# Between attention and the experts: the last tile's jobs first, blank rows on three queues, later biases, more idle transposes

## The chip, the cores and the metric

One core of one Trainium2 chip runs the whole kernel. The metric is the time of one execution on the device in microseconds (us); a profiled execution also has a span, from its first to its last instruction. The engines are PE (TensorE), DVE (VectorE), ACT (ScalarE), POOL (GpSimd) and SP (SyncE); SP, ACT and POOL issue DMAs.

## What is computed

A layer of graph attention and a layer of experts, for N = 4096 nodes of width D = 512, all in float32:

```python
def layer(x, adj, Wks, Wqs, Wvs, Wo, Wg, bg, W1, b1, W2, b2):
    n = layernorm(x)
    q, k, v = (einsum('nd,hdk->hnk', n, W) for W in (Wqs, Wks, Wvs))   # 8 heads of 64
    s = einsum('hqk,hmk->hqm', q, k) * 64 ** -0.5
    s = s + 0.01 * eye - 1e16 * (1 - maximum(adj, eye))                # mask
    x = x + einsum('hqm,hmk,hko->qo', softmax(s), v, Wo)
    f = layernorm(x)
    logits = f @ Wg + bg                                               # 8 experts
    top, idx = top_k(logits, 2)
    w = softmax(top)
    y_e = gelu(f @ W1[e] + b1[e]) @ W2[e] + b2[e]                      # for each expert e
    return x + sum over the two chosen experts of w * y_e
```

## The kernel before

`_fast` works in stages, with P = 128 rows to a tile and 32 tiles (i = 0 to 31). Its order of instructions on every engine is that in which the program writes them.

**Projections and lists.** Keys and values of all nodes go to the table `kv_d` in DRAM, queries to `q_d`, and for every tile of queries a list is made of the nodes that it attends to.

**Attention** runs over pairs of steps, `duos`, S of them. For a tile, each step gathers rows of `kv_d` into a ring (POOL), transposes the keys, and computes scores, exponentials and values. After a tile's last pair, `end_of(i, n)` registers what is left to do for it under later step numbers, with `at(n, job)`; the loop over n takes all jobs registered for n after the pair's own work. When the pairs are used up (n >= S), the loop goes on with n until no jobs are left, so from there on only the jobs remain.

For one tile the jobs are: `scale` (division by the softmax sums), `flip_o` (PE transposes to `po`, ACT copy to `oT`), `project` (PE, L823) and `residual` (DVE adds x, L832, the sum is stored to `out`, L834, and its statistics are taken). Routing follows, by groups of tiles: tiles 0 to 27 go four at a time, then group 7 is tiles 28 and 29, group 8 is tile 30 and group 9 is tile 31. `route(g, n)` registers `root` (one over the standard deviation, DVE), `norm` (ACT, scales x in place, L885), `flip` (PE, ACT), `gate` (PE L905, DVE adds the bias, L909), `rank` and `place` (DVE), `number_places` (PE), `keep_places` (DVE, L949), `pick` twice and `weigh` (DVE, one exponential on ACT, L994), `finish` (DVE) and `scatter`: an indirect DMA on POOL (L1012) that writes each row to the place of its expert in the table `xs_d`, twice per tile. A 1x1 memset `tick` stands ahead of each such DMA.

The steps of the last tiles overlap. From S on they hold, in the order of registration:

| step | jobs |
|---|---|
| S | `rank`, `place` of group 7; `norm` of 8; `flip_o` of tile 31 |
| S+1 | `number_places`, `keep_places` of 7; `flip` of 8; `project`, `residual` of 31 |
| S+2 | `pick`, `weigh` of 7; `gate` of 8; `root` of 9 |
| S+3 | `finish` of 7; `rank`, `place` of 8; `norm` of 9 |
| S+4 | `scatter` of tile 28; `number_places`, `keep_places` of 8; `flip` of 9 |
| S+5 | `scatter` of 29; `pick`, `weigh` of 8; `gate` of 9 |
| S+6 | `finish` of 8; `rank`, `place` of 9 |
| S+7 | `scatter` of 30; `number_places`, `keep_places`, `totals` of 9 |
| S+8, S+9, S+10 | `pick`, `weigh`; `finish`; `scatter` of 31 |

**Totals and blank rows.** `xs_d` gives each of E = 8 experts a region of R = 4224 rows. `totals` counts the rows of each expert, computes `ends` (the first free row of each region, one copy per partition with the partition's number added, L958), and writes 128 blank rows behind each region's last row: eight indirect DMAs on POOL (L964), so that the last tile of every expert has defined rows.

**Tables.** After the jobs, DVE and PE work out from the counts, for each of up to 71 row tiles, its expert and its first row, and put them in `table` (L1125 to L1163). A check of the softmax sums follows, which ends in `flag` (L1179).

**Experts.** `fetch(b)` loads the first row's number from `table` into a register of SP and reads 128 rows of `xs_d` (L1204), so it has to wait for all scatters and blank rows. `bb`, the second biases of all experts copied to all partitions (2 MB), is loaded on ACT's queue ahead of them (L1192); it lies where tiles of the stage before lay. `warm` is 36 transposes of the identity, whose result nobody reads (L1210). `turn(b)` transposes the rows (L1215), `hidden(b)` is the first product (L1227), `turn_hidden` transposes it and applies GELU, `second` is the second product (L1251), adds `bb` (L1263), scales and adds the result to `out` with an accumulating indirect DMA on POOL (L1265). 69 row tiles are always run. The experts' weights, W1 and W2, are loaded on SP's queue into the ring as attention leaves it, and the last of them (L1086, `w`) at step S.

Of the kernel before, what the change touches and what calls it, by code (L numbers as in the profile page):

```python
# [20 lines left out]
P = 128  # L21
# [54 lines left out]
def _fast(ctx, tc, dram, flag, x, adj, Wks, Wqs, Wvs, Wo, Wg, bg, W1, b1, W2, b2, out):  # L76
    nc = tc.nc
# [242 lines left out]
    with ExitStack() as s1:  # L320
# [52 lines left out]
        def norm(i):  # L373
            mv, rstd = mvs.pop(i)
            nc.vector.reciprocal(rstd, rstd)
            xns[i] = work.tile([P, D], F32, tag="xn", name=f"xn_{i}")
            nc.vector.tensor_scalar(
                xns[i], xts.pop(i), mv[:, 0:1], rstd, op0=ALU.subtract, op1=ALU.mult
            )
# [249 lines left out]
    with ExitStack() as s2:  # L629
# [45 lines left out]
        rows_ = 0  # L675
        later = {}

        def at(n, job):
            later.setdefault(n, []).append(job)

        def gather(s, x):
            st = steps[s]
# [115 lines left out]
        def end_of(i, n):  # L798

            hold = {}  # L800

            def scale():
                o = os_[i][:, :, : NP * VW].rearrange("p b (h v) -> p b h v", v=VW)
                r = inverses[:, i].rearrange("p (b h) -> p b h", b=2)
                nc.vector.reciprocal(r, o[:, :, :, KD])
                on = mid.tile([P, 2, NP, KD], F32, tag="on", name=f"on_{i}")
                nc.vector.tensor_mul(
                    on, o[:, :, :, :KD], r.unsqueeze(3).to_broadcast([P, 2, NP, KD])
                )
                hold["on"] = on.rearrange("p b h v -> p (b h v)")  # L810

            def flip_o():
                pt = bank(f"po_{i}", [NP, P])
                for c in range(NP):
                    nc.tensor.transpose(pt[:, c, :], hold["on"][:, ts(c, P)], ident)
                oT = mid.tile([P, NP, P], F32, tag="oT", name=f"oT_{i}")
                nc.scalar.copy(oT, pt)
                hold["oT"] = oT

            def project():  # L820
                hold["py"] = bank(f"py_{i}", [D])
                for c in range(NP):
                    nc.tensor.matmul(  # L823
                        hold["py"], hold["oT"][:, c, :], wo[:, c, :],
                        start=(c == 0), stop=(c == NP - 1),
                    )

            def residual():
                g = group_of[i]
                m = groups[g]  # L830
                xi = xs_[i][:, :D]
                nc.vector.tensor_add(xi, xi, hold["py"])  # L832
                queue = nc.sync if i < NT - 3 else nc.scalar
                queue.dma_start(out=out[ts(i, P), :], in_=xi)  # L834
                if g not in gst:
                    gst[g] = small.tile([P, 2, 4], F32, tag="mvg", name=f"mvg_{g}")
                k = m.index(i)
                stats = small.tile([P, nc.vector.BN_STATS_DIM], F32, tag="stats", name=f"sb_{i}")
                nc.vector.bn_stats(stats, xi)
                nc.vector.bn_aggr(gst[g][:, :, k], stats)  # L840

            scale()
            at(n + 1, flip_o)
            at(n + 2, project)
            at(n + 2, residual)
            g = group_of[i]
            if i == groups[g][-1]:
                route(g, n + 3)

        def route(g, n):  # L850
# [32 lines left out]
            def norm(k):  # L883
                xi = xs_[m[k]]
                nc.scalar.activation(  # L885
                    xi[:, :D], xi[:, :D], AF.Identity, bias=hold["shift"][:, k : k + 1],
                    scale=hold["y"][:, k : k + 1],
                )
                nc.gpsimd.iota(xi[:, D : D + 1].bitcast(I32), pattern=[[0, 1]],
                               base=m[k] * P, channel_multiplier=1)  # L890

            def flip(k):
                i = m[k]
                pt = bank(f"px_{i}", [DC, P])
                for c in range(DC):
                    nc.tensor.transpose(pt[:, c, :], xs_[i][:, ts(c, P)], ident)
                xT = mid.tile([P, DC, P], F32, tag="x2T", bufs=2, name=f"x2T_{i}")
                nc.scalar.copy(xT, pt)
                hold["xT", k] = xT

            def gate(k):
                i = m[k]
                pl = bank(f"pl_{i}", [E])
                for c in range(DC):
                    nc.tensor.matmul(  # L905
                        pl, hold["xT", k][:, c, :], wg[:, c, :],
                        start=(c == 0), stop=(c == DC - 1),
                    )
                nc.vector.tensor_add(hold["l"][:, k, :], pl, bg_sb)  # L909
# [44 lines left out]
            def totals():  # L954
                pn = bank("pn", [E])
                nc.tensor.matmul(pn, ones, count, start=True, stop=True)
                ends = tail.tile([P, E], I32, name="ends")
                nc.vector.tensor_add(ends, pn, pad_e)  # L958
                number = tail.tile([P, E], I32, name="number")
                nc.vector.tensor_scalar_add(number, pn, float(P - 1))  # L960
                closing["number"] = number
                for e in range(E):
                    nc.gpsimd.memset(tick, 0.0)
                    s = nc.gpsimd.indirect_dma_start(  # L964
                        out=xs_d,
                        out_offset=bass.IndirectOffsetOnAxis(ap=ends[:, e : e + 1], axis=0),
                        in_=blank, in_offset=None,
                    )
                    for t in scatters:
                        tc.declare_no_dep(s.ins, t.ins, reason="other rows")  # L970
                    scatters.append(s)
# [48 lines left out]
                    tc.declare_no_dep(s.ins, t.ins, reason="other rows")  # L1020
                scatters.append(s)

            at(n, root)
            n += 1
            for k in range(G):
                at(n + k // 2, lambda k=k: norm(k))
                at(n + k // 2 + 1, lambda k=k: flip(k))
                at(n + k // 2 + 2, lambda k=k: gate(k))
            n += (G - 1) // 2 + 3
            at(n, rank)  # L1030
            at(n, place)
            at(n + 1, number_places)
            at(n + 1, keep_places)
            if g == len(groups) - 1:
                at(n + 1, totals)
            at(n + 2, lambda: pick(0))
            at(n + 2, lambda: pick(1))
            at(n + 2, weigh)
            at(n + 3, finish)
            n += 4  # L1040
            for k in range(G):
                for j in range(2):
                    at(n + k, lambda k=k, j=j: scatter(k, j))

        AHEAD = 5
        tick = small.tile([1, 1], F32, bufs=1, name="tick")
# [53 lines left out]
        while n < S or any(k >= n for k in later):  # L1100
            duo(scores, n + 1)
            duo(values, n)
            if n < S:
                end = steps[duos[n][-1]]
                if end["last"]:
                    end_of(end["i"], n)
                    load_xi(end["i"])
                issue(n + 1 + AHEAD, n)
                load_weights(n)
            for job in later.pop(n, []):  # L1110
                job()
            duo(turn, n + 3)
            if n == S:
                s3.close()
                wff = ctx.enter_context(tc.tile_pool(name="wff", bufs=1))
                for k in range(PARTS, DC + HC):
                    load_part(k, wff.tile([P, SW], F32, name=f"w_{k}"))
            n += 1
# [65 lines left out]
    with ExitStack() as s4:  # L1184
# [4 lines left out]
        ps_t = s4.enter_context(tc.tile_pool(name="ps_t", bufs=2, space=PSUM))  # L1189
        ps_y = s4.enter_context(tc.tile_pool(name="ps_y", bufs=2, space=PSUM))  # L1190
        bb = bbp.tile([P, E, D], F32, name="bb")
        nc.scalar.dma_start(  # L1192
            out=bb.rearrange("p e f -> p (e f)"),
            in_=b2.rearrange("e f -> (e f)").partition_broadcast(P),
        )
        rows, es, xTs, hs, hTs = {}, {}, {}, {}, {}

        def fetch(b):
# [7 lines left out]

        def warm():
            pt = ps_t.tile([P, HC, P], F32, tag="t", name="pt_warm")
            for k in range(36):
                nc.tensor.transpose(pt[:, k % HC, :], ident, ident)  # L1210

        def turn(b):
# [58 lines left out]
        def tiles(b0, b1, first=False):  # L1271
            for b in range(b0, min(b0 + 4, b1)):
                fetch(b)
            if first:
                warm()
            turn(b0)
            hidden(b0)
            if b0 + 1 < b1:
                turn(b0 + 1)
            for b in range(b0, b1):  # L1280
                if b + 4 < b1:
                    fetch(b + 4)
                turn_hidden(b)
                if b + 1 < b1:
                    hidden(b + 1)
                if b + 2 < b1:
                    turn(b + 2)
                second(b)
# [560 lines left out]
```

## Time and profile before

| | us |
|---|---|
| three runs | 2100.89, 2109.29, 2114.70 |
| their median | 2109.29 |
| the profiled execution | 2102.14 |
| its span | 2100.4 |
| PE busy in it | 1953.5 (93%) |
| DVE, ACT, POOL busy | 952.8, 794.9, 603.9 |

The profiled execution's own time is 1.7 us more than its span. Times in the trace are counted from the span's start; L12 is line 12 of the kernel. A row of the timeline gives start, duration, engine, line, operation, output<-input and count, and in brackets how long the engine had been idle and what ended that. A name with q behind it (SPq, ACTq) is an engine's instruction queue, on which DMAs are issued. The granted clock is a share of TensorE's full clock.

### The profile page before, as it was taken

To read this page: it belongs to the slowest core of one execution; us is meant where nothing else is said; L and a number is where in the kernel's file an instruction comes from. 1 tells how busy PE (TensorE), PEld (TensorE's weight loads), DVE (VectorE), ACT (ScalarE), POOL (GpSimd) and SP (SyncE) were. 2 spreads that over 40 slices of the span, in tenths; PEclk is the share of its full clock that TensorE was granted. 3 is DMA by queue.
4 is the path that set the end of the run, shared out by engine and by line. 5 is a ranking of instruction groups with operands and counts; after the bars stand their busy time and mean duration, and the time that the engine had idled before them with its cause. 6 is when DMAs were issued, how large, how long until landed. Compare 5 with 4: busy or idle time off the path is not lost. (4 is left out here: it accounts for less than half of the span.)

```text
span 2100.4 us, 59242 instructions
## 1 busy us (share of the span) xinstructions
PE 1953.5 (93%) x25393; PEld 1302.2 (62%) x25393; DVE 952.8 (45%) x2470; ACT 794.9 (38%) x1161; POOL 603.9 (29%) x725
## 2 busy tenths in 40 slices
PE   8899999999998988998989998889579999999996
PEld 4344444448887877877878787778434444444443
DVE  3455556525544554555555554555613232332322
ACT  3233233316554544545545554445212222222221
POOL 2000000025354445354362726341312212222121
PEclk9999999999999999999999999999779999999998
DMA  9877877249787759788595959677834344433432
GB/s 371 261 248 249 260 253 249 81 179 387 239 280 252 261 202 358 237 292 291 194 376 170 366 184 359 222 276 243 306 116 70 68 71 67 70 68 69 70 66 43
DMA packets 181278, 442.30 MB, mean 211 GB/s; under 512 B 28176, under 2 KB 44560, under 8 KB 180880
## 3 DMA queue, kind: packets, MB, share of 16 engines
q0 software_dynamic: 67712, 251.55, 37.7%
q1 hardware_dynamic: 89136, 154.17, 22.7%
q10 hardware_dynamic: 24160, 32.68, 4.4%
q8 instruction: 205, 3.36, 0.6%
q14 instruction: 65, 0.53, 0.1%
HBM read 364.92 MB, written 73.42 MB: 209 GB/s over the span
## 5 line engine op out<-in xcount | busy, mean ns | idle before, releaser
L691 POOL DMA_INDIRECT ring<-kv_d,idx x361 | 396.5, 1098 | 836.6 <-ACT l L298 438.0
L768 DVE SCALAR_TENSOR_TENSOR pr<-t,pr 128x1024 f32<-128x1024 uint16 x238 | 285.1, 1228 | 265.7 <-ACT pr L762 265.7
L755 PE MATMUL ps<-q,kT 64*64 64x64 f32 (+1 forms) x10224 | 306.5, 237 | 27.5 <-issue 19.8
L783 PE MATMUL o<-ring,pr 128*64 128x65 f32 x8640 | 295.0, 225 | 33.2 <-issue 33.0
L720 ACT COPY kT<-pkT 128x512 f32<-128x512 f32 (+1 forms) x270 | 198.6, 783 | 324.6 <-PE pkT L718 315.7
L755 PEld LDWEIGHTS ps<-q,kT 64*64 64x64 f32 (+1 forms) x10224 | 273.0, 148 | 61.9 <-issue 40.6
L783 PEld LDWEIGHTS o<-ring,pr 128*64 128x64 f32 x8640 | 271.7, 139 | 49.3 <-issue 33.6
L762 ACT ACTIVATE pr<-ps 128x1024 f32<-128x1024 f32 x270 | 270.9, 1026 | 58.2 <-PE ps L755 53.3
L1227 PE MATMUL ph<-ring,xT 128*128 x552 | 251.6, 599 | 0.7 <-ACT xT L1217 0.7
L1265 POOL DMA_INDIRECT out_dram<-y,r x69 | 107.4, 1557 | 448.6 <-ACT y L1264 443.9
L718 PE MATMUL pkT<-ident,ring 128*128 128x128 f32 x1572 | 204.6, 279 | 13.4 <-ACT kT L720 6.5
L718 PEld LDWEIGHTS pkT<-ident,ring 128*128 128x128 f32 x1572 | 176.5, 143 | 39.3 <-issue 26.9
L1251 PE MATMUL py_e<-ring,hT 128*128 x414 | 189.2, 593 | 1.6 <-ACT hT L1245 1.6
L1227 PEld LDWEIGHTS ph<-ring,xT 128*128 128x128 f32 x552 | 100.6, 192 | 101.8 <-issue 100.1
L1264 ACT ACTIVATE y<-y,wt 128x512 f32<-128x512 f32 x69 | 49.8, 721 | 246.3 <-DVE y L1263 246.3
L1232 DVE COPY h<-ph 128x512 f32<-128x512 f32 x69 | 47.7, 692 | 200.7 <-PE ph L1227 200.7
L1263 DVE TENSOR_TENSOR y<-py_e,bb 128x512 f32<-128x512 f32 x69 | 47.7, 692 | 194.5 <-PE py_e L1251 194.5
L599 PE MATMUL pv<-wv,xT 128*128 128x512 f32 x256 | 132.5, 613 | 0.0
L599 PE MATMUL pk<-wk,xT 128*128 128x512 f32 x256 | 128.9, 615 | 0.7 <-ACT xT L394 0.7
L584 PE MATMUL pq<-xT,wq 128*128 128x512 f32 x256 | 125.9, 607 | 0.0
L1012 POOL DMA_INDIRECT xs_d<-x,slot_i x64 | 69.4, 1085 | 195.0 <-DVE t L730 89.2
L823 PE MATMUL py<-wo,oT 128*128 128x512 f32 x256 | 122.6, 623 | 0.0
(257 smaller groups left out, 1833.6 us busy)
## 6 DMA issues: line engine op xcount, KB each, us to landing
adj<-in_adj_dram SPq DMA_DIRECT2D x64, 1024.0 KB, 5.7
r<-xs_d SPq DMA_DIRECT2D x69, 258.0 KB, 2.7
kv_d<-kvr ACTq DMA_DIRECT2D x32, 516.0 KB, 5.8
ring<-kv_d SPq DMA_DIRECT2D x32, 516.0 KB, 6.8
ring<-in_L_ffn_W_dram SPq DMA_DIRECT2D x56, 256.0 KB, 5.3
xt<-in_x_dram SPq DMA_DIRECT2D x32, 256.0 KB, 6.1
q_d<-qT ACTq DMA_DIRECT2D x32, 256.0 KB, 2.7
q<-q_d SPq DMA_DIRECT2D x32, 256.0 KB, 5.6
```

The source lines that it names most:

```text
L584: nc.tensor.matmul(pq, w["q"][:, c, ts(p, P)], xTs[b][:, c, :], start=(c == 0), stop=(c == DC - 1),)
L599: nc.tensor.matmul(pk, xTs[b][:, c, ts(t, P)], w[n][:, c, :], start=(c == 0), stop=(c == DC - 1),)
L691: nc.gpsimd.indirect_dma_start(out=g, out_offset=None, in_=kv_d, in_offset=bass.IndirectOffsetOnAxis(ap=idx[i // GL][:, i % GL, a : a + 1] ...
L718: nc.tensor.transpose(pk[:, x * NP + p, :], g[:, ts(p, P)], ident)
L720: nc.scalar.copy(kT[:, : nk * NP], pk[:, : nk * NP])
L755: nc.tensor.matmul(ps[c : c + nk, r, p * P + x * nq : p * P + (x + 1) * nq], kT[r * KD : (r + 1) * KD, p, c : c + nk], q[r * KD : (r + 1) ...
L762: nc.scalar.activation(pr.rearrange("p h q -> p (h q)"), ps.rearrange("p r f -> p (r f)"), AF.Exp)
L768: nc.vector.scalar_tensor_tensor(pr, st["t"].unsqueeze(1).to_broadcast([P, H, P]), 0.0, pr, op0=ALU.is_gt, op1=ALU.mult,)
L783: nc.tensor.matmul(o[c * HALF : (c + 1) * HALF, h // NP, (h % NP) * VW : (h % NP + 1) * VW], pr[:, hd * NP + p, c * HALF : (c + 1) * HALF] ...
L823: nc.tensor.matmul(hold["py"], hold["oT"][:, c, :], wo[:, c, :], start=(c == 0), stop=(c == NP - 1),)
L1227: nc.tensor.matmul(ph, xTs[b][:, c, :], wparts[c][:, bass.ds(es[b], 1), :], start=(c == 0), stop=(c == DC - 1),)
L1251: nc.tensor.matmul(py, hTs[b][:, c, :], wparts[DC + c][:, bass.ds(es[b], 1), :], start=(c == 0), stop=(c == HC - 1),)
```

## The change

Four edits, all between the last pair of attention and the first row tile of the experts.

1. Jobs are registered with their tile, and from step S on the jobs of a step are sorted so that later tiles come first (those of one tile keep their order).
2. Of the eight blank writes, those of experts 0 to 2 stay indirect DMAs on POOL. For 3, 4 and 5 SP, and for 6 and 7 ACT, loads the row number from `ends` into a register and issues a plain DMA to that address.
3. `bb` is loaded on SP's queue, behind the fetches of the first four row tiles.
4. `warm` has 60 transposes.

```diff
-        def at(n, job):
-            later.setdefault(n, []).append(job)
+        def at(n, i, job):
+            later.setdefault(n, []).append((i, job))
...
-            at(n + 1, flip_o)
-            at(n + 2, project)
-            at(n + 2, residual)
+            at(n + 1, i, flip_o)
+            at(n + 2, i, project)
+            at(n + 2, i, residual)
...
                 for e in range(E):
-                    nc.gpsimd.memset(tick, 0.0)
-                    s = nc.gpsimd.indirect_dma_start(
-                        out=xs_d,
-                        out_offset=bass.IndirectOffsetOnAxis(ap=ends[:, e : e + 1], axis=0),
-                        in_=blank, in_offset=None,
-                    )
+                    if e < 3:
+                        nc.gpsimd.memset(tick, 0.0)
+                        s = nc.gpsimd.indirect_dma_start(
+                            out=xs_d,
+                            out_offset=bass.IndirectOffsetOnAxis(ap=ends[:, e : e + 1], axis=0),
+                            in_=blank, in_offset=None,
+                        )
+                    else:
+                        eng, queue = (
+                            (mybir.EngineType.SP, nc.sync) if e < 6
+                            else (mybir.EngineType.Activation, nc.scalar)
+                        )
+                        last = nc.values_load(
+                            ends[0:1, e : e + 1], engines=(eng,), min_val=e * R,
+                            max_val=e * R + N,
+                            skip_runtime_bounds_check_because="counts of at most N",
+                        )
+                        s = queue.dma_start(out=xs_d[bass.ds(last, P), :], in_=blank)
...
-            at(n, root)
+            at(n, m[-1], root)
...
-            for job in later.pop(n, []):
+            todo = later.pop(n, [])
+            if n >= S:
+                todo.sort(key=lambda job: -job[0])
+            for _, job in todo:
                 job()
...
         bb = bbp.tile([P, E, D], F32, name="bb")
-        nc.scalar.dma_start(
-            out=bb.rearrange("p e f -> p (e f)"),
-            in_=b2.rearrange("e f -> (e f)").partition_broadcast(P),
-        )
...
         def warm():
             pt = ps_t.tile([P, HC, P], F32, tag="t", name="pt_warm")
-            for k in range(36):
+            for k in range(60):
                 nc.tensor.transpose(pt[:, k % HC, :], ident, ident)
...
             for b in range(b0, min(b0 + 4, b1)):
                 fetch(b)
             if first:
+                nc.sync.dma_start(
+                    out=bb.rearrange("p e f -> p (e f)"),
+                    in_=b2.rearrange("e f -> (e f)").partition_broadcast(P),
+                )
                 warm()
```

The other calls of `at` in `route` get `m[-1]`, the last tile of the group, in the same way.

More of the change, by code (lines that the diff above doesn't have):

```diff
@@ L1021, in scatter @@
                 scatters.append(s)
-            at(n, root)
+            at(n, m[-1], root)
             n += 1
             for k in range(G):
-                at(n + k // 2, lambda k=k: norm(k))
-                at(n + k // 2 + 1, lambda k=k: flip(k))
-                at(n + k // 2 + 2, lambda k=k: gate(k))
+                at(n + k // 2, m[-1], lambda k=k: norm(k))
+                at(n + k // 2 + 1, m[-1], lambda k=k: flip(k))
+                at(n + k // 2 + 2, m[-1], lambda k=k: gate(k))
             n += (G - 1) // 2 + 3
[L1030 to L1033, printed above, removed]
+            at(n, m[-1], rank)
+            at(n, m[-1], place)
+            at(n + 1, m[-1], number_places)
+            at(n + 1, m[-1], keep_places)
             if g == len(groups) - 1:
[L1035 to L1039, printed above, removed]
+                at(n + 1, m[-1], totals)
+            at(n + 2, m[-1], lambda: pick(0))
+            at(n + 2, m[-1], lambda: pick(1))
+            at(n + 2, m[-1], weigh)
+            at(n + 3, m[-1], finish)
             n += 4
@@ L1042, in route @@
                 for j in range(2):
-                    at(n + k, lambda k=k, j=j: scatter(k, j))
+                    at(n + k, m[-1], lambda k=k, j=j: scatter(k, j))
         AHEAD = 5
```

## The prediction

> **What bounds the kernel now.** I read the summary of the page, then its 40 slices. PE is at 8 or 9 tenths nearly everywhere, with one hollow at slices 29 and 30 (about 1500 to 1560 us), between attention and the experts. All four edits lie there, so the forecast is the length of that hollow.
>
> ```profile
> PE   8899999999998988998989998889579999999996
> PEclk9999999999999999999999999999779999999998
> ```
>
> The timeline of PE over the hollow shows where the time stands:
>
> ```profile
> 1490.52 0.64 PE L815 MATMUL po<-ident,on 128*128 128x128 f32 x4
> ...
> 1496.10 5.38 PE L823 MATMUL py<-wo,oT 128*128 128x512 f32 x8
> ...
> 1522.65 0.37 PE L1148 MATMUL pej<-diag,ones 128*128 128x256 bf16 x1 [5.87 <-DVE diag L1143]
> 1526.18 0.16 PE L1178 MATMUL pb<-badb,ones 128*128 128x1 bf16 x1 [3.16 <-DVE badb L1176]
> 1526.59 5.99 PE L1210 MATMUL pt_warm<-ident 128*128 128x128 f32 x36 [0.24 <-DVE flag L1179]
> 1542.92 1.09 PE L1215 MATMUL pt_e<-ident,r 128*128 128x128 f32 x4 [10.35 <-DMA r<-xs_d]
> 1544.69 6.76 PE L1227 MATMUL ph<-ring,xT 128*128 x8 [0.68 <-ACT xT L1217]
> 1551.28 0.60 PE L1215 MATMUL pt_e<-ident,r 128*128 128x128 f32 x4
> ```
>
> Attention's last matmuls end near 1488.8. The last tile's output is projected from 1496.10, the idle transposes end at 1532.58, and PE then waits 10.35 us for the first expert rows. From 1551.28 on it has no gap: the stage view from there to 2067.52 has PE busy 515.84 of 516.24 us. So whatever brings the second tile's transposes (1551.28) forward comes off the end one for one, and that is the mark I forecast.
>
> What holds the rows back stands in POOL's timeline:
>
> ```profile
> 1527.03 0.96 POOL L964 DMA_INDIRECT xs_d<-blank,ends  x1 [0.22 <-issue]
> 1527.99 0.09 POOL L1011 MEMSET tick<- 1x1 f32 x1
> 1530.21 0.95 POOL L1012 DMA_INDIRECT xs_d<-x,slot_i  x1 [2.12 <-issue]
> 1531.15 0.09 POOL L1011 MEMSET tick<- 1x1 f32 x1
> 1531.46 0.96 POOL L1012 DMA_INDIRECT xs_d<-x,slot_i  x1 [0.23 <-issue]
> ```
>
> The last tile's two scatters stand behind eight blank writes, one each 1.27 us (1518.12 to 1527.03 in seven steps), and a stall of 2.12 us. The last lands at 1534.3. SP's waits agree, and its timeline shows the fetches and the biases starting together:
>
> ```profile
> SPq L1204 <- DMA xs_d<-x,slot_i: 9.0, 1, 9.0
> ```
>
> ```profile
> 1534.71 4.14 SPq L1204 DMA_DIRECT2D r<-xs_d  x5
> 1534.71 0.36 ACTq L1192 DMA_DIRECT2D bb<-in_L_ffn_b_dram  x1
> ```
>
> The first row tile of 258 KB then takes 7.8 us, beside a 2 MB load; the page's median for such a fetch is 2.7 us.
>
> The last tile's own chain is held earlier, in ACT's timeline:
>
> ```profile
> 1493.70 0.81 ACT L885 ACTIVATE x<-x,shift,root 128x512 f32<-128x512 f32 x1 [9.70 <-DVE same L922]
> 1494.42 0.56 ACT L817 COPY oT<-po 128x512 f32<-128x512 f32 x1
> ...
> 1503.06 0.35 ACTq L834 DMA_DIRECT2D out_dram<-x  x1
> ...
> 1508.58 0.81 ACT L885 ACTIVATE x<-x,shift,root 128x512 f32<-128x512 f32 x1 [3.13 <-DVE x L1008]
> ```
>
> The copy of `oT` was ready at 1491.2 and stands behind tile 30's normalization. That one scales x in place, so it waits until the store of the same x has landed (issue 1487.58, landing 1493.6). Tile 31 repeats it: store at 1503.06, normalization 5.52 us later. The releasers named in brackets are not what counts: on ACT's queue the wait just ahead of each normalization is one on a landing.
>
> **What the skill says.** "TensorE: Matmul & The Clock Gate", section "What's actually happening": the clock is half after an idle window of about 3.4 us and full after a busy one, with free-running windows. The trace agrees: granted 0.50 from 1508 to 1530, full in 1532 to 1534, 0.50 again from 1538, and the eight matmuls of the first expert tile took 6.76 us where the later ones take 3.60. "DMA: Bandwidth & Descriptors", section "SWDGE vs HWDGE vs iDMA": POOL builds descriptors in software, SP and ACT have hardware for it. The trace agrees: 0.96 us of POOL for one blank, 0.34 us of SP for one fetch of the same size. The same page, "Issuing engines are not separate DMA queues", says that the transfers still share 16 engines; the 7.8 us beside `bb` agree.
>
> **The order of jobs.** S is the number of attention pairs; at steps from S on, tile 31's jobs now precede those of tiles 28 to 30.
> 1. `oT` at S: the transposes end at 1491.16, so the copy (0.56) ends at 1491.8. Projection: 3.60 us at full clock, as in the projection at 1483.16; PE idles only 0.7 us before, so I keep the full clock. 1491.9 to 1495.5, against 1501.5 before.
> 2. Residual: `rank` and `place` of group 7 hold DVE until 1495.5, so the add (0.69) ends at 1496.3.
> 3. The store: in the trace such issues wait for earlier landings while the weights stream (SP's L1086 waited 5.9 us in 7 waits; this store 0.8 us after its add). I take 0.9 again: issue 1497.2, landing 5.5 later, 1502.7. On ACT the exponential of group 7 comes first: statistics 0.9, `keep_places` 0.15, `root` 2.5, the gate add 0.15, `pick` 2.25 on DVE, to 1502.25, plus 0.2. Normalization at 1502.75, 5.8 earlier than before.
> 4. Normalization start to the logits' add took 5.23 us before (1508.58 to 1513.81), 0.6 of it PE behind group 8's numbering, which now comes after. 4.65 gives 1507.4, the sum 1507.55.
> 5. A loss: `gate` of tile 31 now stands ahead of group 8's `pick` on DVE, which waits behind it. So after 1507.55 follow `pick` and the difference 2.15, `rank` and `place` 1.8, `finish` of group 8 0.95, `keep_places` and `totals` 0.55: `ends` at 1513.0, against 1516.99. Net gain 4.0.
> 6. From `ends` to the flag, before 9.54 us of small DVE work: 1522.55. The warm transposes start there.
>
> **The blank rows.** POOL keeps three blanks, then tile 30's two scatters and tile 31's two, which are ready by about 1516.5: seven at 1.27. The first starts 0.75 after `ends` (so long did POOL need after a wait, 1514.86 to 1515.60): the seventh at 1513.75 + 6 x 1.273 = 1521.4, landing 2.9 later (as 1531.46 to 1534.3), SP's issue 0.37 after that: 1524.65. Before: 1534.71. The stall of 2.12 coincides with one 16 KB packet of the instruction queue (1528.39); with ten POOL instructions fewer it should fall after these scatters. Zero, else 2.1. On SP three register loads and writes at about 0.9 us each (the pitch of its fetches) run in its wait for `table`; behind them are only the fetches. On ACT two such pairs take some 2 us; behind them stands the last exponential, due 2.3 us after `ends`. At most 0.3, taken as nothing. A write from SP or ACT to an address in a register is not in the trace: the fetches in the other direction land in 2.6 to 7.8 us, and by 1524 it has 6 or more. No gain below nothing; a loss only if landing takes over 8.
>
> **Biases behind the rows.** The first rows then travel without the 2 MB: 2.7 to 5.2 us after 1524.65, so 1527.4 to 1529.9. `bb` starts near 1528 and needs about 8.4 as before: 1536.5. Its first reader (L1263) comes 9.2 us after the first expert matmuls end, near 1545.5, so it is hidden by 9 us. The fifth fetch behind it is needed only at about 1550.
>
> **More transposes.** 36 took 5.99 us: 0.213 each at half clock for some 3.8 us, then 0.107. Full clock comes 3.4 to 6.8 us after the start, as the windows fall; I take 5.1: 24 x 0.213 + 36 x 0.107 = 8.95, so they end at 1531.5 (1530.6 to 1532.4). That is after the rows, so the transposes now set the start; a late row up to 1531.5 costs nothing. The clock stays full: 0.60 transposes, 0.7 copy and hand-over, eight matmuls 3.55: the mark is at 1536.4.
>
> **Sum.** 1551.28 - 1536.4 = 14.9 us. Span 2100.4 gives 2085.5, and 2102.14 of the profiled execution 2087.2. The median of the runs shown, 2109.29, lies 7.15 above that execution, so in such runs I expect 2109.29 - 14.9 = 2094.4 us.
>
> **Rivals.**
> - The store doesn't move: its issue stays in line with the weights until 1502 or so. For it: that line ran at 389 to 399 GB/s up to 1508; against: SP issued weights at several points between 1495 and 1499. The normalization then comes near 1507, and step 5's loss remains, so `ends` is at 1517.4. The gain is 14.9 - 4.4 = 10.5: 2098.8.
> - The rows come after the transposes: POOL's stall stays (2.1) and eight blanks with four scatters crowd the DMA engines, landing at 1534. For it: 12 x 264 KB in 9 us is 350 GB/s. The gain is 14.9 - 2.5 = 12.4, or 9 if the clock falls as well: 2097 to 2100.
> - Slower: the writes at register addresses on SP and ACT land so late that every fetch waits for them. For it: no such write is in the trace; against: the fetches and stores of this size. The mark stays at 1551.28 if they land at about 1535, 20 us after issue; at 30 us the first rows come 8 us later than before on a cold PE: 2109.29 + 6 = 2115.
>
> **How the numbers follow.** Forecast 0.66, store 0.18, late rows 0.12, slower 0.04. The three fast cases lie between 2094 and 2100. The runs of before spread over 13.8 us, so I take 2083 to 2104. About 1% (21 us) is what a measurement of this kernel can tell from no change; the forecast is 0.7%. By the runs' spread about four in ten of the forecast's own chance and little of the others' may show as over 1%: faster 0.27, same 0.68, slower 0.05.
>
> **What would show it.** Right: L823 of the last tile before 1496 (by this trace's time) in 3.6 us, `ends` some 4 us earlier, three L964 on POOL, the fetch near 1524.6, L1210 x60 with no PE wait for `r` behind it, first L1227 at 3.6 us. Wrong: a wait for `r` after the transposes, L885 of the last tile still near 1508, or a DVE wait for `bb` at L1263.

## The result

The changed kernel took 2091.61 us (median of six runs, 2082.94 to 2094.52), the kernel before 2106.44 (six runs): a ratio of 0.9932 with a 95% interval of 0.9911 to 0.9953, about 14 us. In a later comparison it was 0.9944 (0.9924 to 0.9964), about 12 us. The forecast was 2094.4.

The profiled executions differ by less: span 2092.2 against 2100.4. The stage view says why. I call the stretch from the gate matmuls of tiles 28 and 29 (L905 x16, which begin within 0.2 us of attention's last values) to the second row tile's transposes the *hollow*. Of the kernel before:

```profile
1488.71:1551.28 62.57, 27.39 (x113) 18.44 (x110) 25.12 (x154) 5.95 (x11) 22.54 (x45) 0.65 0.67 251
1551.28:2100.40 549.12, 531.31 (x1645) 261.72 (x1643) 160.41 (x345) 125.60 (x206) 107.42 (x69) 0.99 0.38 65
```

and of the changed kernel (stretch, its length, then busy time of PE, PEld, DVE, ACT and POOL, granted clock, DMA share, GB/s):

```profile
1493.30:1543.29 49.99, 26.34 (x138) 19.79 (x134) 25.44 (x154) 6.06 (x11) 15.70 (x30) 0.69 0.85 310
1543.29:2092.20 548.91, 531.31 (x1645) 261.63 (x1643) 160.36 (x345) 125.67 (x206) 107.44 (x69) 0.99 0.38 65
```

The hollow shrank by 12.58 us, POOL's work in it by 6.8; the experts behind it take the same time to 0.2 us. But attention, which the change does not touch, ended 4.6 us later in this execution. Over all 14 traces of this study that moment lay between 1483.6 and 1498.3. So the time of one execution cannot tell edits of 2 to 5 us apart. The hollow is free of this scatter (two traces of the changed kernel gave 49.99 and 49.60), but it has a smaller one of its own, which the table below shows. All times below that are counted from the start of the hollow are written as "+".

PE's timeline of the changed kernel:

```profile
1493.30 1.95 PE L905 MATMUL pl<-wg,x2T 128*128 128x8 f32 x16
1495.11 0.64 PE L815 MATMUL po<-ident,on 128*128 128x128 f32 x4
1496.47 5.40 PE L823 MATMUL py<-wo,oT 128*128 128x512 f32 x8 [0.73 <-ACT oT L817]
...
1518.84 0.19 PE L956 MATMUL pn<-count,ones 128*128 128x8 bf16 x1 [0.24 <-DVE more L1012]
...
1529.52 9.00 PE L1221 MATMUL pt_warm<-ident 128*128 128x128 f32 x60 [0.24 <-DVE flag L1194]
1538.36 0.60 PE L1226 MATMUL pt_e<-ident,r 128*128 128x128 f32 x4
1539.75 3.70 PE L1238 MATMUL ph<-ring,xT 128*128 x8 [0.80 <-ACT xT L1228]
1543.29 0.60 PE L1226 MATMUL pt_e<-ident,r 128*128 128x128 f32 x4
```

The wait for `r` (10.35 us before) is gone: the first rows' transposes follow the 60 idle ones without a gap, and the first expert product runs at full clock. The rows were ready near +41.5 (the fetch at +38.3 and the 3.2 us that rows take without the biases beside them, an estimate from the runs below), the transposes ended at +45.2. What ends last ahead of the experts is now the idle transposes themselves. POOL's and SP's queues:

```profile
1522.56 0.96 POOL L965 DMA_INDIRECT xs_d<-blank,ends  x1 [0.21 <-issue]
1523.51 0.09 POOL L1023 MEMSET tick<- 1x1 f32 x1
1523.82 0.96 POOL L1024 DMA_INDIRECT xs_d<-x,slot_i  x1 [0.23 <-ACT gelu L1138]
...
1527.60 0.99 POOL L1024 DMA_INDIRECT xs_d<-x,slot_i  x1 [0.23 <-issue]
```

```profile
1520.49 2.66 SPq L980 DMA_DIRECT2D xs_d<-blank  x3
1531.61 2.92 SPq L1215 DMA_DIRECT2D r<-xs_d  x4
1534.64 0.36 SPq L1286 DMA_DIRECT2D bb<-in_L_ffn_b_dram  x1
```

Three blanks, four scatters and no stall on POOL; the fetch stands at +38.3 (1531.61 - 1493.30), against +46.0 before (1534.71 - 1488.71), and the biases behind it.

### The profile page after: what moved, and what is told of

It reads as the page before. It is cut to its first block, busy times and chain, and to the rows that moved or that the text cites. A ratio compares the mean times of both kernels' runs of the same rounds, so it can differ in the third digit from the quotient of the medians.

```text
span 2092.2 us, 59301 instructions
## 1 busy us (share of the span) xinstructions
PE 1952.9 (93%) x25417; PEld 1303.8 (62%) x25417; DVE 953.2 (46%) x2470; ACT 795.3 (38%) x1161; POOL 598.3 (29%) x715
## 3 DMA queue, kind: packets, MB, share of 16 engines
q0 software_dynamic: 67312, 250.23, 37.9%
## 5 line engine op out<-in xcount | busy, mean ns | idle before, releaser
L783 PEld LDWEIGHTS o<-ring,pr 128*64 128x64 f32 x8640 | 273.2, 140 | 51.7 <-issue 36.2
L718 PEld LDWEIGHTS pkT<-ident,ring 128*128 128x128 f32 x1572 | 176.8, 143 | 38.3 <-issue 26.1
L1274 DVE TENSOR_TENSOR y<-py_e,bb 128x512 f32<-128x512 f32 x69 | 47.7, 692 | 194.5 <-PE py_e L1262 194.5
L1243 DVE COPY h<-ph 128x512 f32<-128x512 f32 x69 | 47.7, 692 | 189.7 <-PE ph L1238 189.7
```

The source lines that it names most:

```text
L718: nc.tensor.transpose(pk[:, x * NP + p, :], g[:, ts(p, P)], ident)
L783: nc.tensor.matmul(o[c * HALF : (c + 1) * HALF, h // NP, (h % NP) * VW : (h % NP + 1) * VW], pr[:, hd * NP + p, c * HALF : (c + 1) * HALF] ...
```

## The experiments

All are read by the hollow. In the table, "store" is how long after the end of its add the store of tile 31's x was issued, "ends" the start of the instruction that computes `ends`, "warm" the start and end of the idle transposes, "fetch" the first fetch of rows (L1204 before), "start" the first rows' transposes, "first product" the length of the first expert product. c_norm, c_all and c_best are three further versions, described at the end of this section. The six versions "order alone", "biases alone", "60 transposes alone", "old order", "old blanks" and "old biases" ran once each, under the profiler, so no ratio of times is given for them.

| kernel | store | ends | warm | fetch | start | first product | hollow |
|---|---|---|---|---|---|---|---|
| before | 0.8 | 28.1 | 37.9 to 43.9 | 46.0 | 54.2 | 6.8 | 62.6 |
| order alone | 0.0 | 24.4 | 34.0 to 40.1 | 44.0 | 52.3 | 5.9 | 59.8 |
| blanks alone | 0.3 | 28.1 | 38.1 to 44.0 | 39.4 | 49.5 | 5.8 | 56.8 |
| biases alone | 1.0 | 28.3 | 38.1 to 44.2 | 46.1 | 49.3 | 6.0 | 57.0 |
| 60 transposes alone | 0.3 | 27.5 | 37.2 to 45.6 | 45.3 | 53.7 | 6.4 | 61.7 |
| changed | 2.2 | 26.3 | 36.2 to 45.2 | 38.3 | 45.1 | 3.7 | 50.0 |
| changed, old order | 0.0 | 28.8 | 38.7 to 47.6 | 40.0 | 47.4 | 3.7 | 52.4 |
| changed, old blanks | 0.0 | 24.3 | 34.0 to 42.8 | 44.0 | 47.2 | 6.8 | 55.7 |
| changed, old biases | 2.1 | 24.8 | 34.5 to 43.8 | 36.9 | 46.1 | 6.6 | 53.9 |
| changed, 36 transposes | 0.8 | 25.0 | 34.7 to 41.5 | 37.1 | 41.4 | 3.7 | 46.3 |
| changed, second trace | 1.2 | 25.7 | 35.4 to 44.8 | 37.9 | 44.7 | 3.7 | 49.6 |
| c_norm | 0.0 | 24.3 | 34.0 to 40.0 | 36.3 | 39.8 | 3.7 | 44.7 |
| c_all | 0.0 | 21.8 | 34.6 to 40.5 | 34.7 | 40.3 | 3.7 | 45.2 |
| c_best | 0.0 | 22.8 | 32.7 to 39.5 | 35.4 | 39.3 | 3.7 | 44.3 |

Six of these traces are of programs that are the same up to `ends`: order alone, both traces of the changed kernel, and the changed kernel with the old blanks, the old biases or 36 transposes. Their `ends` comes anywhere from +24.3 to +26.3, because the projection takes from 3.70 to 5.40 us and the store then waits 0.0 to 2.2 us; in all six `ends` follows the issue of the store by 14.8 to 15.1 us. So a difference of up to 2 us between two hollows need not come from the edit; the column `ends` tells. The order itself stands out of this scatter: the five traces with the old order have `ends` at +27.5 to +28.8.

**Each edit alone.** The theory (T in the expectations) is that rows and idle transposes run beside each other and the later one sets PE's start; its rival (U), that each edit is worth what it saves on its own step.

The order:

```diff
+            if n >= S:
+                todo.sort(key=lambda job: -job[0])
```

> The order of jobs alone, on the kernel before. Read as the hollow: from the gate matmuls of tiles 28 and 29, where attention's last values end, to the second row tile's transposes (62.6 us before, 50.0 after). Theory T, the rows and the transposes are in parallel and the later one sets PE's start: here the rows set it, through POOL. ends comes 2.3 us earlier as in the changed kernel, but all eight blank writes then stand ahead of four scatters: 0.75 + 12 x 1.27 + landing, so the fetch moves up by 0 to 2 us and the hollow is 60.6 to 62.6. Rival U, the edits add up by what each does to its own step: 2.3 off, 60.3.

Hollow 59.8, 2.8 off, 0.8 below the theory's range and 0.5 below the rival's number. `ends` came 3.7 earlier, not 2.3. The fetch moved by 2.0, the upper end of what the theory allowed; the other 0.8 is a shorter first product, because the clock rose at another point of it. This run alone does not decide.

The blank rows:

```diff
-                    nc.gpsimd.indirect_dma_start(...)
+                    if e < 3: ... else: values_load on SP or ACT, queue.dma_start(...)
```

> The blank rows on three queues alone, on the kernel before. T: POOL is then at the last scatter 8 us earlier, the fetch at about 1526.5 on the clock of the trace before, the rows beside bb 7.8 later at 1534.3, just after the 36 transposes (1533.3), so PE keeps its clock: the hollow is about 50.5, nearly all of the change's gain, and the time 12 us shorter, ratio 0.994. U: only the shorter POOL queue, 8 us: hollow 54.5, ratio 0.996.

Hollow 56.8, ratio 0.9962 (0.9947 to 0.9978). Both numbers of the theory were missed; the rival was 2.3 off in the hollow and right in the ratio. The fetch came at +39.4, 6.7 earlier, but the rows then took 10.1 us, so PE waited and lost its clock:

```profile
1529.82 5.94 PE L1222 MATMUL pt_warm<-ident 128*128 128x128 f32 x36 [0.24 <-DVE flag L1191]
1541.22 1.09 PE L1227 MATMUL pt_e<-ident,r 128*128 128x128 f32 x4 [5.46 <-DMA r<-xs_d]
1542.98 5.77 PE L1239 MATMUL ph<-ring,xT 128*128 x8 [0.68 <-ACT xT L1229]
```

The part of the theory that stands is that the rows are the later ones; its size does not: part of what POOL saved went into the load of `bb` beside the rows and into the clock.

The biases:

```diff
-        nc.scalar.dma_start(out=bb, ...)          # ahead of the fetches
+                nc.sync.dma_start(out=bb, ...)    # behind four fetches
```

> The biases behind the rows alone, on the kernel before. T: the fetch stays at 1534.7, the rows land 3 to 5 us later instead of 7.8, so PE waits 5 to 7 us behind its transposes and falls to half clock as before: hollow 58 to 60. U: the same 3 to 5 us. Both tell only how long the rows take without the 2 MB beside them.

Hollow 57.0, 5.5 off and 1 below the expected range. The fetch did not move (+46.1); the rows needed 3.2 us in place of 8.2, the low end of what was expected, and the first product took 6.0 and not 6.8:

```profile
1535.43 2.96 SPq L1200 DMA_DIRECT2D r<-xs_d  x4
1538.88 0.34 SPq L1271 DMA_DIRECT2D bb<-in_L_ffn_b_dram  x1
```

```profile
1538.63 1.09 PE L1211 MATMUL pt_e<-ident,r 128*128 128x128 f32 x4 [5.14 <-DMA r<-xs_d]
1540.52 5.95 PE L1223 MATMUL ph<-ring,xT 128*128 x8 [0.80 <-ACT xT L1213]
```

The transposes:

```diff
-            for k in range(36):
+            for k in range(60):
```

> 60 idle transposes alone, on the kernel before. T: they end 3 us later (1535.6) while the rows land at 1542.5, so nothing is delayed; if the idle rest of about 7 us still holds an idle clock window the first expert product stays at 6.8 us and the hollow at 62.6, else it is 59. U: the 3.2 us of the full clock are gained, 59.4.

Hollow 61.7, 0.9 off. They ended at +45.6, the rows came at +53.7, and after the rest of 8.1 us half clock was back. The 0.9 is where the clock's steps fell: the last tile's projection, which this edit does not reach, took 4.75 us (5.38 before), and the first product 6.40 (6.76). Alone, this edit is worth about nothing.

The four savings add up to 2.8 + 5.7 + 5.5 + 0.9 = 14.9; together they gave 12.6 to 13.0. That is not the plain sum of independent steps either, as the next four runs show.

**Each edit taken back.**

```diff
-            for k in range(60):
+            for k in range(36):
```

> The changed kernel with 36 idle transposes instead of 60. T (the later of rows and transposes sets PE's start): the fetch is at 1531.6 on the clock of the changed kernel's trace and the rows need 3.1 us, as they did with the biases behind them alone, so they are there at 1534.7; 36 transposes end near 1535.5. PE starts 2.8 us earlier at full clock: hollow 47.2 against 50.0, the 60 cost time. Rival W, the longer warming is needed: PE falls to half clock, hollow 50 or more.

```profile
1528.23 6.83 PE L1221 MATMUL pt_warm<-ident 128*128 128x128 f32 x36 [0.24 <-DVE flag L1194]
1534.89 0.60 PE L1226 MATMUL pt_e<-ident,r 128*128 128x128 f32 x4
1536.29 3.70 PE L1238 MATMUL ph<-ring,xT 128*128 x8 [0.80 <-ACT xT L1228]
```

Hollow 46.3, 3.7 less than with 60, and still at full clock: the theory's case, by more than it said. The excess is no work of this edit: in this trace the transposes began 1.5 us earlier (+34.7 and not +36.2). What 24 transposes cost is read from their own length, 6.83 us against 9.00 and 9.43: 2.2 to 2.6 us. The fourth edit costs that much once the other three are in. In time it is not resolved: 0.9936 of the kernel before (0.9917 to 0.9956), where the changed kernel had 0.9932 and 0.9944.

```diff
+        nc.scalar.dma_start(out=bb, ...)          # ahead of the fetches again
```

> The changed kernel with the biases back on ACT's queue ahead of the rows. T: beside the 2 MB the rows take 8 to 10 us (10 with the blank rows alone), so they land at 1539.5 to 1541.6 while 60 transposes end at 1538.4: PE waits 1 to 3 us without losing its clock, hollow 51 to 53.5. Rival U (each edit is worth what it was alone, 5.5): 55.5.

Hollow 53.9, 3.9 more; the rows took 9.1 us, to +46.1, and PE waited 2.27 us. The theory had the wait right and the clock wrong, and the sum was 0.4 above its range. The windows of this kernel around the wait (columns as above):

```profile
1538.01:1541.43 3.42, 3.42 (x33) 3.42 (x32) 0.00 (x0) 0.00 (x0) 0.00 (x0) 1.00 0.92 365
1541.43:1544.84 3.41, 1.14 (x11) 0.85 (x8) 0.00 (x0) 0.00 (x0) 0.00 (x0) 1.00 0.93 356
1544.84:1551.66 6.82, 6.14 (x9) 2.53 (x8) 0.00 (x0) 0.58 (x1) 0.00 (x0) 0.50 0.02 8
```

A stretch of 3.41 us with PE busy for 1.14 was enough for half clock in the next.

```diff
-            if n >= S:
-                todo.sort(key=lambda job: -job[0])
```

> The changed kernel with the jobs in the old order. T: the transposes still set the start; they begin 38.1 us into the hollow, as with the blank rows alone, instead of 36.2, so hollow 51.9. The rows land at 42.5 and have 4 us to spare. U: 2.8 as alone, 52.8.

Hollow 52.4 (51.9 expected). The fetch at +40.0 has time to spare, and the order works through the start of the transposes alone: +38.7 instead of +36.2 or +35.4.

```diff
-                    if e < 3: ... else: values_load on SP or ACT, queue.dma_start(...)
+                    nc.gpsimd.indirect_dma_start(...)
```

> The changed kernel with all eight blank writes on POOL. T: the fetch is 44 us into the hollow, as with the order alone, rows at 47.1; the transposes begin at 34 and end at 43, so the rows set the start after a wait of 4 us: hollow 52 at full clock, 55 if the clock falls. U: 5.7 as alone, 55.7.

Hollow 55.7. The rows came at +47.2 after a fetch at +44.0, PE waited 4.38 us and fell to half clock (first product 6.8 us). The rival's 55.7 fits the number, the theory's "55 if the clock falls" the mechanism; the trace has both the wait and the clock.

So, from the changed kernel: blanks 5.7, biases 3.9, order 2.4, and the 60 transposes minus 2.2 to 2.6. Blanks and biases are if anything too small here: `ends`, ahead of both, came 2.0 and 1.5 us earlier in those two traces than in the changed kernel's first. Blanks and biases are worth this much only because a late row also costs the clock, about 3 us. The case in which the 60 transposes would help, a PE that waits for its rows, is the one that the other edits removed.

**What else is in the hollow.** In the changed kernel ACT shows why the last tile gained less than forecast:

```profile
1504.83 0.35 ACTq L834 DMA_DIRECT2D out_dram<-x  x1
1505.28 0.59 ACT L898 COPY x2T<-px 128x512 f32<-128x512 f32 x1 [5.58 <-DVE rt L872]
1509.25 0.20 ACT L1006 ACTIVATE less<-less 128x2 f32<-128x2 f32 x1 [3.39 <-DVE less L1005]
1510.15 0.81 ACT L885 ACTIVATE x<-x,shift,root 128x512 f32<-128x512 f32 x1 [0.70 <-DMA out_dram<-x]
```

The store's issue came 2.2 us after the add had ended (1502.65); the trace puts its wait down to a weight load of SP's queue (L1098), which landed at 1504.76. The normalization waits first for group 7's exponential and then for that store. Where the store hardly waited, with the old blanks, the normalization followed directly on the exponential, and still began only at +15.0 (1503.91 - 1488.87):

```profile
1498.25 0.35 ACTq L834 DMA_DIRECT2D out_dram<-x  x1
...
1503.80 0.20 ACT L994 ACTIVATE less<-less 128x2 f32<-128x2 f32 x1 [4.52 <-DVE less L993]
1503.91 0.80 ACT L885 ACTIVATE x<-x,shift,root 128x512 f32<-128x512 f32 x1
...
1513.21 0.15 DVE L958 TENSOR_TENSOR ends<-pn,pad_e 128x8 int32<-128x8 f32 x1
```

Three versions, all with 36 transposes, change this.

```diff
+                if m[k] == NT - 1:
+                    xi = xs_[m[k]] = mid.tile([P, W], F32, tag="x", bufs=10, name="xlast")
                 nc.scalar.activation(
-                    xi[:, :D], xi[:, :D], AF.Identity, ...
+                    xi[:, :D], xo[:, :D], AF.Identity, ...        # xo: the tile that is stored
...
-            at(n + 2, m[-1], weigh)                               # pick and finish likewise
+            at(n + 2 + back, m[-1], weigh)                        # back = 1 for group 7
```

> The changed kernel with 36 idle transposes, tile 31 normalized into another buffer (so that ACT need not wait until the store of its x has landed), and group 7's pick and exponential moved one step back, behind that normalization. With 36 transposes and nothing else the last normalization starts 15.7 us into the hollow, root is done at 12.5, and the hollow is 46.3. Theory N, the store's landing and the exponential ahead hold tile 31: the normalization starts at 12.7, the logits are there at 18 (after group 7's finish on DVE), ends 2.3 us earlier, hollow 44. Rival D, DVE's own work is the limit by now: normalization early, hollow 46.

Hollow 44.7, between the theory's 44 and the rival's 46. The normalization starts at +12.9 (expected 12.7) and not +15.7: the store's landing and the exponential ahead did hold it. But the gain went no further. `ends` came at +24.3, 14.9 us after the store's issue as in the six traces above, and no earlier than with the order alone and with the old blanks, whose stores waited as little as this one. The logits came 6.5 us after the normalization, since group 7's exponential now stands between it and the copy of its transposes and waits for `pick`. The 1.6 us against 36 transposes alone are 0.7 from an earlier `ends`, where the store of that trace had waited 0.8 longer, and 0.8 from idle transposes of 6.00 and not 6.83 us. So a gain of this version is not shown.

```profile
1502.43 0.35 ACTq L834 DMA_DIRECT2D out_dram<-x  x1
1505.93 0.81 ACT L887 ACTIVATE xlast<-x,shift,root 128x512 f32<-128x512 f32 x1 [2.46 <-DVE l L911]
1509.81 0.20 ACT L1008 ACTIVATE less<-less 128x2 f32<-128x2 f32 x1 [3.07 <-DVE less L1007]
1509.92 0.57 ACT L900 COPY x2T<-px 128x512 f32<-128x512 f32 x1
...
1517.33 0.16 DVE L960 TENSOR_TENSOR ends<-pn,pad_e 128x8 int32<-128x8 f32 x1
```

```diff
+            back = 1 for group 7, 2 for group 8; group 8's finish behind the totals
-        blank rows: three on POOL, three on SP, two on ACT
+        blank rows: five on SP, and three on ACT behind the last exponential
```

> As c_norm, and group 8's pick and finish moved behind the totals, all blank writes off POOL: five on SP, three on ACT behind the last exponential. N: ends moves to 20.3 us into the hollow (24.7 with 36 transposes alone), the last scatter to about 29.2 and the fetch to 33, rows at 36; but the same DVE work stands ahead of the flag, so the transposes begin at 31.7 and end near 38: hollow 43, and time 6 to 7 us under the changed kernel's. Rival: the three late writes on ACT land last and the rows set the start, 44 or more.

Hollow 45.2, 2 more than expected and no better than c_norm. `ends` came at +21.8 (expected 20.3) and the fetch at +34.7, early as meant, but the transposes began at +34.6 and not +31.7. The exponential of group 7 stood between tile 31's normalization and the copy of its transposes, as it did in c_norm, and group 8's `pick` and `finish` lengthen the way from `ends` to the transposes, 12.9 us against 9.7 in c_norm. The rows were ready, the start was not. The rival's number fits, its reason does not: the rows did not set the start.

```diff
-            at(n + 2 + back, m[-1], weigh)
+            at(n + 2 + 2 * back, m[-1], weigh)                    # on c_norm
```

> As c_norm, and group 7's exponential stands behind the copy of tile 31's transposes on ACT (in c_norm and c_all it stands between tile 31's normalization and that copy and waits for pick, so the logits came 6.5 us after the normalization's start and not 4.6). Theory: the gate's matmuls of tile 31 end 17.5 us into the hollow instead of 19.4, DVE is ready for them at 18.2, ends and the transposes come 1.2 us earlier, hollow 43.6 against 44.7. Rival, group 7's finish then takes the same time from the same chain on DVE: 44.7. In time neither can be told from c_norm; against the kernel before 0.991.

Hollow 44.3. `ends` came 1.45 earlier than in c_norm, at +22.8, with the store and the projection alike in both traces. So the place of the exponential, and not DVE's own work, had held `ends` in c_norm. The transposes began at +32.7, 1.3 earlier as expected, but took 6.83 us and not 6.00, since full clock came 5.5 us after their start and not 3.8:

```profile
1499.99 0.81 ACT L887 ACTIVATE xlast<-x,shift,root 128x512 f32<-128x512 f32 x1 [2.47 <-DVE l L911]
1501.60 0.58 ACT L900 COPY x2T<-px 128x512 f32<-128x512 f32 x1 [0.80 <-PE pp L945]
1503.95 0.20 ACT L1008 ACTIVATE less<-less 128x2 f32<-128x2 f32 x1 [1.76 <-DVE less L1007]
...
1509.93 0.15 DVE L960 TENSOR_TENSOR ends<-pn,pad_e 128x8 int32<-128x8 f32 x1
...
1519.78 6.83 PE L1224 MATMUL pt_warm<-ident 128*128 128x128 f32 x36 [0.24 <-DVE flag L1197]
1526.45 0.60 PE L1229 MATMUL pt_e<-ident,r 128*128 128x128 f32 x4
```

In time: c_norm 0.9934 (0.9910 to 0.9958), c_all 0.9935 (0.9910 to 0.9960), c_best 0.9914 (0.9885 to 0.9942), each against the kernel before. By the hollow c_best is 18 us shorter than the kernel before and 5 to 6 shorter than the changed one, 2.2 to 2.6 of it from the transposes; in time its interval overlaps with that of the changed kernel, so only the first of the two is shown by time. The second trace of the changed kernel:

> The changed kernel once more, beside the two: how far the hollow varies from execution to execution (50.0 in its first trace). If it is within 1 us, differences of 2 us between single traces can be read; if the rows, the store or the clock fall otherwise, by 2 to 3.

Hollow 49.6, 0.4 from the first. That is closer than the parts are: the transposes began 0.8 earlier and took 0.4 longer. With the table's spread of `ends`, 2 us between two hollows can be put down to an edit only where the steps that it touches moved by as much; the 0.4 us between c_best and c_norm can not be read, the 1.45 of their `ends` can.

## Why the prediction was right

The time lies in the range, the direction is right, and 14.9 us were forecast where the times give 14 (12 in the later comparison) and the hollow 12.6 to 13.0. The mechanism held: the wait for the rows went, and the idle transposes set PE's start. That the number came so near is in part luck: the interval of the ratio is about 10 to 19 us, and in the steps two terms were too small and one too large. Step by step, in the time from the hollow's start:

1. *`oT` at S.* The copy moved as said (+3.1). The projection did not run at full clock: 5.40 us and not 3.60. This term was 1.8 too small. Of the nine traces with the new order one, with the old biases, shows it at full clock (3.70).
2. *Residual.* Starts at +8.7 and not +6.9, all of it from step 1.
3. *The store.* It waited 2.2 us for an earlier landing, not 0.9: the second term that was too small. The program does not fix this wait: it is 1.2 in the second trace of the same kernel, and 0.0 to 2.1 in the others with the new order. The normalization began at +16.9, forecast +14.0, before +19.9: 3.0 earlier, not 5.8. The first rival (the store does not move) was wrong in its strict form, but half of its loss came true.
4. *To the logits.* The sum began 4.63 after the normalization; 4.65 was forecast.
5. *The loss behind `gate`.* Real: logits to `ends` 4.8 (forecast 5.45, before 3.0). `ends` came 1.8 earlier by its own start, where 4.0 was forecast; the 2.2 missing are the 2.8 of steps 1 to 3 less the 0.6 that this step took less than forecast. With the order alone and with the old blanks, where the store did not wait, `ends` came 3.7 to 3.8 earlier: there the forecast of 4.0 is nearly right, with a slow projection (5.40 us) and a shorter step 5 that cancel in part.
6. *`ends` to the flag.* 9.9 from there to the first warm transpose, as against 9.8. The two register loads and writes on ACT stayed hidden: the last exponential followed its input by 0.2 us in both kernels.

The two starts of `ends` in step 5, before and in the changed kernel:

```profile
1516.82 0.17 DVE L958 TENSOR_TENSOR ends<-pn,pad_e 128x8 int32<-128x8 f32 x1 [0.22 <-PE pn L956]
```

```profile
1519.61 0.16 DVE L958 TENSOR_TENSOR ends<-pn,pad_e 128x8 int32<-128x8 f32 x1
```

*The blank rows.* The fetch came 12.0 after `ends`, forecast 11.65. The stall of 2.12 us is gone, as forecast, but its cause is open. It stood ahead of tile 31's first scatter, 2.12 to 2.14 us long, in all five kernels whose POOL program has the old number of instructions, and in none with fewer. The instruction queue's packet lay within 0.4 us of its beginning in three of them and 2.2 and 2.5 us ahead of it in the other two, so that packet alone does not explain it. No experiment took it away by itself. The writes of SP and ACT delayed the fetch little: from the last scatter's start to the fetch it was 4.0 us in the changed kernel, 4.8 with the blanks alone, 3.3 before. Whether the difference comes from the crowding of the DMA engines was not tested. The rival that made the kernel slower had no part in it.

*Biases.* Rows 3.2 us without the 2 MB beside them, as read from two kernels in which PE waits for them; the first reader of `bb` (L1263 before, L1274 in the changed kernel) waits for PE and not for `bb`.

*More transposes.* 9.00 us, forecast 8.95, and they do set the start. What the prediction did not draw from this is the sign: by its own numbers 36 would have ended before or with the rows, near 1528.5. The run with 36 showed 2.2 to 2.6 us lost to the other 24.

*Sum.* The mark came at +50.0 where +47.7 was forecast. The 2.3 us are `ends` but for 0.1; the rest of the chain held.

## What to carry to other kernels

When several edits shorten parallel paths to one start, work out each path's end after all of them: the edit that fills a wait is the first to become the wait. Count the traces from the last event that the change cannot reach, since the scatter ahead of it (15 us here) hides gains of some microseconds, and look at what else differs between two traces before a difference is put down to the edit: one store's wait moved `ends` by up to 2 us here. And a step that starts earlier is not yet a gain. Another buffer for an operation in place behind a store, with an exponential moved from ahead of it, brought tile 31's normalization from +15.0 to +12.9, and nothing of it reached `ends` until the exponential was moved once more.

## What the runs showed of the hardware

- In these traces the granted clock changes at multiples of 3.41 us from its last change (half clock from 1496.58 to 1499.99 in the changed kernel, one time 3.41, and from 1506.82 to 1534.13, eight times). The stretches here are cut at these points. A wait of 2.27 us, in such a stretch with PE busy for a third of it, was followed by half clock and cost 3 us in the first product (changed kernel, old biases). The Trainium skill, "TensorE: Matmul & The Clock Gate", section "What's actually happening", puts half clock after at least one idle window of about 3.4 us; here a window that was idle for two thirds was enough.
- PE's busy time does not decide it alone. In the changed kernel a stretch with 2.68 of 3.41 us busy, most of it gate matmuls of eight columns, was followed by half clock:

```profile
1493.17:1496.58 3.41, 2.68 (x29) 2.37 (x25) 2.18 (x12) 0.59 (x1) 2.76 (x7) 1.00 1.04 341
1496.58:1499.99 3.41, 3.41 (x5) 1.33 (x6) 2.96 (x17) 0.81 (x1) 1.59 (x5) 0.50 1.03 404
```

  With the old biases the boundary fell elsewhere, the stretch held the same 2.68 us, most of it projection, and the projection ran through in 3.70 us. What is counted was not tested.

```profile
1500.46:1503.87 3.41, 2.68 (x9) 1.25 (x8) 2.96 (x19) 1.33 (x2) 2.80 (x5) 1.00 0.98 371
1503.87:1507.29 3.42, 1.79 (x10) 0.91 (x8) 3.15 (x13) 0.07 (x1) 1.45 (x5) 1.00 1.04 410
```

- A 2 MB load from 16 KB, copied to all partitions, that was issued beside a 258 KB fetch lengthened it from 3.2 to between 8.2 and 10.1 us.
- A register load and a plain write to that address take SP 0.85 to 1.45 us from one to the next, against 1.27 of POOL for an indirect one.
